# Key projections of a cross-attention kernel: whole block products in four banks instead of Strassen's products with a chain of reads

## The chip, the cores and the metric

The kernel runs on one core of one Trainium2 chip. The metric is the device time of one execution in microseconds (us); before the change the median of three runs is 1877.12 us (1876.99 to 1877.57). Engines are named as in the profile: PE is TensorE (PEld its weight loads), DVE is VectorE, ACT is ScalarE, POOL is GpSimd, SP is SyncE, which issues most DMAs.

## The reference

For each of B = 32 batches, x and ctx (here y) are 256 x 1024 (channels C x positions N):

```
x_q = w_qk y            (as N x C)        x_k = w_qk x          x_v = w_v x + b_v
energy = x_q x_k        (N x N)           attention = softmax over the last axis
attention = attention / (1e-7 + its sum over the rows)
x_r = x_v attention     (C x N)           out = x + relu(w_t (x - x_r) + b_t)
```

## The kernel before

**What is computed.** The kernel folds weights once, at the start. The query and the key share w_qk, so it forms G = -(w_qk^T w_qk) and multiplies only x by it; these 256 x 1024 products are called the keys. The energies of a batch are then y^T times its keys, with their sign turned, so that exp takes a scale of -1. Likewise w_t w_v is folded into the values, and w_t x is a product of its own, the x product.

**Forms.** Full precision is had from two reduced-precision forms of every operand, HIGH and LOW (the rounded value and the rest). A product of 128 x 128 by 128 x 512 is three matmuls in ORDER: high by high, high by low, low by high. The second needs the right operand's LOW form, the third the left operand's. HIGH forms are made by ACT (copy with rounding), LOW forms by POOL or DVE (a subtraction).

**Strassen's products.** Keys, x product and each of four energy groups (E0 to E3, 256 rows each) are 2 x 2 block products done with seven block products P1 to P7 instead of eight. `chain` (line 335) makes the words `kP1` to `kP7`, `xP1` to `xP7` and `E0P1` to `E3P7`. The partial sums P1, P1 + P6 and P1 + P6 + P7 grow in one bank, "a", and each is copied out by ACT (`r1`, `r2`, `r3`) before the next product may add to it; DVE joins a copy with bank "b" or "c" (`c11`, `c22`, `c12`, `c21`); P3 goes into bank "c" once `c22` has read it.

**Keys (lines 344 to 383).** KB puts the key's a, b and c into banks 2, 0 and 1. `kc11`, `kc22` write blocks 11 and 22 to `sums`, `kc12` leaves block 12 in its bank, block 21 is in bank 2 after P4. Then follow the forms of what the energies read: `khD`, `klD` for blocks 11 and 22, `kh21`, `kl21` for block 21, and four sums `kT1` to `kT4` with their forms `kTh0`, `kTl0` (of T1 and T3) and `kTh1`, `kTl1` (of T2 and T4). Of these `kT1`, `kT3`, `kT4` and `kl21` are on DVE, `kT2`, `klD`, `kTl0` and `kTl1` on POOL, the rest on ACT.

**Banks.** There are eight PSUM banks. Energies use 0 to 3 (a = 3, b = 0, c = 1, d = 2). A row tile n of 128 rows has its 1024 energies in banks 2 and 3 (n odd) or 0 and 1 (n even): `exp{n}` on ACT in place with the row sum, `ri{n}` on DVE, and for each half h `h{n}{h}` (HIGH of the probabilities, ACT), `l{n}{h}` (LOW, DVE) and `sum{n}{h}` (share of the column sum, DVE). When those three have read a half, its bank is free. Banks 4 to 7 take the values (`V..`, 12 matmuls of 256 columns each), the x product, and then the attention products `A{n}{c}{h}` (three matmuls each). The key products of batch b+1 are made at the end of batch b, and so have to wait for the last tiles, 6 and 7, to leave banks 0 to 2.

**Order.** The order of all work is written out by hand as words in three texts: FIRST (batch 0), STEADY (batches 1 to 29, with + and - for words of the next and the last batch) and LAST. Each engine executes its words in the order of the text (`InOrder`, line 51); waits between engines follow from the data. `ldx`, `ldy` and `st` are DMAs on SP's queue, `add` one on POOL's. Loads go through a ring of two buffers (`raws`), sums through one of four, reads through one of four (`rs`). `ys..`, `yl..`, `ysl..`, `xl..`, `xTl..` and `join..` are POOL's other work, `yh..`, `ysh..`, `xh..`, `xTh..`, `pos..` ACT's; `cols`, `inv`, `turn`, `div..` (DVE) make the column sums and divide by them.

**Batch 0** makes its keys another way: `first_keys` (line 578) multiplies whole blocks by the untransformed forms of G, `gt`, in four banks at once (words `FHH0` to `FHL1`), while `left_blocks("G", ...)` makes the seven left operands that Strassen's products need from batch 1 on (words `Gs1` to `GlS`). `whole` (line 589) makes a block of the first energies and x products from six matmuls: three forms by two halves of the contraction. `Ssq` multiplies w_v by w_t for the values, `Swtc` copies the turned w_t that it reads.

Of the kernel before, what the change touches and what calls it, by code (L numbers as in the profile page):

```python
# [17 lines left out]
def kernel(  # L18
# [135 lines left out]
    def graw():  # L154
        return split(rs["g"])


    gt, tt = (
        efs["weights"][:, j].rearrange("p h (k c) -> p h k c", k=KC) for j in range(FORMS)
    )  # L160
# [68 lines left out]
    for k in range(KC):  # L229
        once(f"Sgh{k}", act.mul, gt[:, HIGH, k], g_bank[:, k], -1.0)  # L230
    once(
        "Sgl", dve.scalar_tensor_tensor, gt[:, LOW], g_bank, -1.0, value(gt[:, HIGH]),
        ALU.mult, ALU.subtract,
    )
    once("Sgraw", lambda: act.mul(graw(), g_bank, -1.0))
# [342 lines left out]
    def first_keys(j, m, k):  # L578
        for i in range(KC):
            for h in range(MH):  # L580
                matmul(
                    (kb["b"], kb["c"], kb["a"], banks[:, 3])[2 * i + h],
                    gt[:, j, k, ts(i, P)],
                    xf[:, m, 2 * k + h],
                    (j, m, k) == (HIGH, HIGH, 0),
                    (j, m, k) == (LOW, HIGH, 1),
                )

    def whole(into, left, right):
        for j, m in ORDER:  # L590
            for k in range(KC):
                matmul(
                    into, left(j, k), right(m, k),
                    (j, m) == ORDER[0] and k == 0, (j, m) == ORDER[-1] and k == KC - 1,
                )
# [25 lines left out]
    forms("k11", lambda j: g(j, K11), kb["b"])  # L621
    forms("k22", lambda j: g(j, K22), banks[:, 3])
    forms("k12", lambda j: k12[:, j], kb["c"])
    words["Fraw11"] = lambda b: act.copy(sums["k", b][:, 0], kb["b"])
    words["Fraw22"] = lambda b: act.copy(sums["k", b][:, 1], banks[:, 3])
# [121 lines left out]
    for c in range(KC):  # L747
# [19 lines left out]
        FX11 E1P6 h01 Gs1 yl10 h00 E1r2 FX00 kTl0 E1P7 +ldx0 l00 l01 l10 Fxw1 sum00 E1r3
        E1P5 E1P4 +xh0 E1c22 Gs2 E1c21 E1P2 Fxw0 E1P3 A100 Gl12 Gs4 Ts1 yl11 exp3 E1c11
        Gs3 Ts3 ri3 E1c12 h31 ysl1 Ts2 exp2 A110 l31 sum31 A101 +ldx1 A010 A111 +xl0 GhS
        ri2 E2P1 h21 A001 E2r1 sum30 sum21 l21 h20 E2P6 +xT3 Ts4 +xT1 l20 +ldy0 E2P5 E2r2  # L770
        h30 sum20 l30 E2P7 E2P2 E2P4 E2r3 A011 +xh1 E2c22 E2P3 +xT2 A301 GlS A000 A201
        A300 E2c21 A311 E2c11 exp5 ri5 E2c12 h51 l51 sum51 exp4 +yh01 ri4 E3P1 sum50 h41
        E3r1 h40 +xT4 h50 A211 E3P6 E3r2 l41 sum41 l40 l50 E3P5 E3P7 +xTh1 E3r3 E3P4 sum40
        E3P2 A310 E3c22 E3c21 E3P3 +xTh0 +xl1 +ys01 +ys02 +yl01 A210 +ys04 +xTl1 exp7
        +yh00 E3c11 A511 ri7 +ldy1 E3c12 h70 exp6 l70 sum70 ri6 A510 A200 A501 ThS h61
        +kP1 sum71 A410 l61 +kr1 sum61 +kP6 +xTl0 h60 +ys03 +kr2 +ysh0 TlS +kP5 sum60 +kP7
        A401 l60 +kP2 +ys11 +kr3 +yl00 cols +kc22 +kP3 A411 A500 +kc11 +kc12 +ys12 h71
        +ysl0 +kP4 +ys14 A400 +khD +yh10 +kT1 +ys13 l71 +kT2 A701 +klD +kT4 inv +kT3 A710
# [21 lines left out]
        -kTh1 -kh21 -kTh0 -yh11 --A700 -E0P1 -E0r1 -kTl1 --A611 --A600 -E0P6 -kTl0 -ysl1  # L800
        --turn --A610 -kl21 -E0P2 -E0r2 -E0P7 -E0P5 --div0 -E0r3 -E0P4 --div1 -E0c11 -yl11
        -E0c22 -E0c21 -exp1 -ri1 -yl10 -V11 -E0P3 -h11 -h10 -E0c12 -sum11 -l11 -V10 -l10
        -exp0 -vh1 -ri0 -V01 -E1P1 -sum10 -E1r1 -h01 -V00 -vl1 -l01 -sum01 --join0 -E1P6
        -vh0 -E1r2 -h00 -xP1 -E1P4 -E1P7 --join1 -vl0 ldx0 -l00 -E1P5 -sum00 xh0 -xP2
        -A111 -E1r3 -E1c22 -E1P2 -E1c21 -xr1 --pos0 -E1c11 -xc11 -exp3 -xP6 -E1P3 -xr2
        -ri3 xT1 -xP5 -xP7 -A011 -A100 -h31 -E1c12 -sum31 -l31 -exp2 -h30 -ri2 -xr3 -E2P1
        -A311 -h21 -E2r1 -xP4 -E2P6 -sum30 -l30 -xc22 -xP3 -sum21 -l21 xl0 --add0 xT2 xT3
        -E2P4 -h20 -xw21 -E2r2 -E2P7 -xc12 -l20 -sum20 xh1 -E2r3 -E2P5 -E2c22 xT4 -A110
        xTh1 -E2c21 -E2P2 -E2c11 xl1 -exp5 -E2P3 -A101 -ri5 -A000 -A010 -h51 -A001 -A300
        -E2c12 -sum51 -exp4 -l51 -ri4 -h40 -E3P1 -h41 -E3r1 xTh0 -A200 -A310 -sum50 -l40  # L810
        -l41 -sum41 ldy0 ldy1 -E3P6 -E3r2 -E3P5 -sum40 ys03 -E3P7 -h50 ys11 yh00 ys01
        -A210 xTl1 -l50 -E3P4 -E3r3 --pos1 -E3c22 -E3c21 -exp7 -A301 -E3P2 -E3c11 -ri7
        -E3P3 yl00 ys02 xTl0 -E3c12 ys04 yh10 -h70 -A510 -A500 -A211 -A201 --add1 -sum70
        -l70 -exp6 -ri6 kP1 -sum71 -h60 -A511 -h61 -A410 -sum61 ys13 kr1 yh01 -h71 -l61
        kP6 -l71 -l60 kr2 --st1 yl01 Zx0 --st0 -sum60 kP5 kP7 -A411 ysh0 kr3 ysl0 kP2 kc22
        kc11 kP3 kc12 khD -A400 -A710 kP4 kT1 -A610 -A501 -A711 -A401 kT3 -cols kT2 klD
# [61 lines left out]
```

## Time and profile before

| | |
|---|---|
| median of three runs | 1877.12 us |
| the profiled execution | 1876.58 us, its span 1874.5 us |
| PE busy | 1861.9 us, 8680 matmuls |
| weight loads (PEld) | 1506.3 us |
| DVE, ACT, POOL busy | 1596.7, 1439.3, 1407.3 us |
| granted TensorE clock, mean | 0.999 |
| DMA | 136.75 MB, mean 73 GB/s |

Times in rows of the profile are us; the mean of one instruction is ns. A row of the order of time has start, duration, engine, line, operation, tiles written <- read, and count; a bracket gives the idle time before it and what ended that. In a group, the number behind the second bar is the idle time before its instructions and what ended most of it. All kernel work goes through one helper, so its line is L62 and groups are told apart by tiles: `xf,gws` are the keys, `gf,ysum` and `gf,yd` the energies, `xf,tws` the x product, `vws,xf` the values, `efs,uf` the attention. Matmuls are pipelined, so that the duration shown for one (some 390 ns) is longer than the step from one to the next.

### The profile page before, as it was taken

How to read it: one execution, taken by the hardware profiler on the slowest of the kernel's cores; microseconds unless marked ns; L12 is line 12 of the kernel's file. 1: busy time of each engine (PE TensorE's matmuls, PEld its weight loads, DVE VectorE, ACT ScalarE, POOL GpSimd, SP SyncE). 2: the span in 40 equal slices, each digit the busy share in tenths (PEclk: the TensorE clock that was granted, in tenths of full speed). 3: DMA queues.
4: the chain of work that ended last, by engine and by line, in shares of the span. 5: the costliest groups of instructions: out<-in, count | busy, mean ns of one | idle time of the engine just before them, and what ended most of it. 6: DMA issues, size and time to landing. Idle time of an engine off the chain costs nothing.

```text
span 1874.5 us, 25084 instructions
## 1 busy us (share of the span) xinstructions
PE 1861.9 (99%) x8680; PEld 1506.3 (80%) x8680; DVE 1596.7 (85%) x3044; ACT 1439.3 (77%) x2223; POOL 1407.3 (75%) x975
## 2 busy tenths in 40 slices
...
GB/s 97 39 76 90 58 89 57 68 90 68 80 68 60 88 75 72 68 68 79 90 58 79 57 79 90 57 89 53 74 91 60 88 56 68 90 68 79 74 62 68
DMA packets 46719, 136.75 MB, mean 73 GB/s; under 512 B 4480, under 2 KB 5376, under 8 KB 46592
## 3 DMA queue, kind: packets, MB, share of 16 engines
...
## 4 chain that ended last, share of the span: by engine, by line
PE 94%; DVE 2%; ACT 1%; issue 1%; POOL 1%; DMA 0%; DVEq 0%; ACTq 0%
PE banks L62 94%; DVE sums L62 1%; ACT rs L62 1%; POOL xf L62 0%; DVE banks L62 0%; POOL sums L62 0%; ACT banks L62 0%; DVE acc L62 0%; DVE efs L62 0%; DMA z<-in_L_xattn_w_qk_dram 0%; POOL raws L62 0%; ACT efs L62 0%; POOL z L62 0%; POOL yd L62 0%; DMA out_dram<-z 0%
## 5 line engine op out<-in xcount | busy, mean ns | idle before, releaser
L62 PE MATMUL banks<-efs,uf 128*128 128x512 f32 x3072 | 771.7, 390 | 0.0
L62 PEld LDWEIGHTS banks<-efs,uf 128*128 128x128 f32 x3072 | 576.5, 188 | 124.6 <-ACT xe L62 0.3
L62 ACT COPY rs<-banks 128x512 f32<-128x512 f32 (+1 forms) x475 | 279.2, 588 | 202.5 <-PE banks L62 193.1
L62 PE MATMUL banks<-gf,ysum 128*128 128x512 f32 x1524 | 415.1, 394 | 0.0
L62 DVE SCALAR_TENSOR_TENSOR efs<-banks,small,efs 128x512 fp32r<-128x512 f32 x512 | 374.5, 742 | 11.2 <-ACT efs L62 9.7
L62 ACT ACTIVATE efs<-banks,small 128x512 fp32r<-128x512 f32 x512 | 340.0, 690 | 43.7 <-DVE small L62 31.8
L62 ACT ACTIVATE banks<-banks,small 128x1024 f32<-128x1024 f32 x256 | 279.2, 1091 | 82.8 <-DVE small L62 79.1
L62 DVE SCALAR_TENSOR_TENSOR acc<-banks,small,acc 128x512 f32<-128x512 f32 x448 | 325.1, 743 | 17.5 <-ACT efs L62 15.2
L62 PEld LDWEIGHTS banks<-gf,ysum 128*128 128x128 f32 x1524 | 276.7, 188 | 72.2 <-ACT rs L62 14.9
L62 PE MATMUL banks<-gf,yd 128*128 128x512 f32 x1158 | 330.4, 397 | 0.5 <-DVE acc L62 0.2
L62 DVE CUSTOM_DVE_ANT_0 banks<-banks,rs 128x512 f32<-128x512 f32 x254 | 178.6, 703 | 117.3 <-PE banks L62 81.9
L62 POOL TENSOR_TENSOR sums<-raws 128x256 f32<-128x256 f32 (+1 forms) x188 | 190.1, 1064 | 116.7 <-DMA raws<-in_ctx_dram 116.6
L62 PEld LDWEIGHTS banks<-gf,yd 128*128 128x128 f32 x1158 | 207.8, 188 | 62.1 <-issue 10.4
L62 POOL TENSOR_TENSOR gf<-sums,gf 128x1024 fp32r<-128x1024 f32 x95 | 227.3, 2408 | 2.3 <-ACT gf L62 0.2
L62 POOL TENSOR_TENSOR xf<-sums,xf 128x1024 fp32r<-128x1024 f32 x62 | 147.9, 2408 | 97.6 <-ACT xf L62 97.5
L62 PEld LDWEIGHTS banks<-vws,xf 128*128 128x128 f32 x1536 | 196.6, 190 | 8.2
L62 DVE CUSTOM_DVE_ANT_0 banks<-banks,rs,small 128x512 f32<-128x512 f32 x254 | 192.2, 757 | 11.8
L62 PE MATMUL banks<-vws,xf 128*128 128x256 f32 x1536 | 198.7, 282 | 0.0
L62 POOL TENSOR_TENSOR z<-z,xe 128x1024 f32<-128x1024 f32 x62 | 149.1, 2405 | 61.8 <-DVE z L62 61.8
L62 PE MATMUL banks<-xf,gws 128*128 128x512 f32 x651 | 179.6, 407 | 4.1 <-DVE sums L62 0.4
L62 PE MATMUL banks<-xf,tws 128*128 128x512 f32 x651 | 173.3, 390 | 0.0
L62 POOL TENSOR_TENSOR ysum<-sums,ysum 128x1024 fp32r<-128x1024 f32 x64 | 154.6, 2416 | 21.5 <-ACT ysum L62 21.5
...
## 6 DMA issues: line engine op xcount, KB each, us to landing
...
```

What stands on the lines that cost most here:

```text
L62: self.last = getattr(self.engine, name)(*args, **kwargs)
```

## The change

The keys of batches 1 to 31 are made as whole blocks: `key_product(i, h)` makes block (i+1, h+1) from six matmuls (words `kD11`, `kD12`, `kD21`, `kD22`), each in a bank of its own: KB is now 11 in bank 2, 12 in bank 0, 21 in bank 1, 22 in bank 3. No partial sum is read on the way. ACT copies blocks 11 and 22 to `sums` (`kraw11`, `kraw22`); `kT1`, `kT3` read block 12 from bank 0, `kT4`, `kh21`, `kl21` block 21 from bank 1. Batch 0 uses the same banks and the same forms of G, kept now in `gws`, and the seven left operands of G are no longer made. All three orders are written anew.

```diff
-    gws = mem.tile([P, FORMS, LEFTS, P], F32R, name="gws")
+    gws = mem.tile([P, FORMS, KC, C], F32R, name="gws")
...
-    once("Sgraw", lambda: act.mul(graw(), g_bank, -1.0))
...
-    left_blocks("G", gws, graw)
     left_blocks("T", tws, lambda: wtT)
...
-    KB = dict(a=2, b=0, c=1)
-    chain("k", KB, lambda i: lambda j: gws[:, j, LEFT[i]], lambda i: lambda m: xf[:, m, RIGHT[i]])
+    def whole(into, left, right):
+        for j, m in ORDER:
+            for k in range(KC):
+                matmul(
+                    into, left(j, k), right(m, k),
+                    (j, m) == ORDER[0] and k == 0, (j, m) == ORDER[-1] and k == KC - 1,
+                )
+
+    KB = {11: 2, 12: 0, 21: 1, 22: 3}
     kb = {w: banks[:, at] for w, at in KB.items()}
+
+    def key_product(i, h):
+        whole(
+            kb[10 * (i + 1) + h + 1],
+            lambda j, k: gws[:, j, k, ts(i, P)],
+            lambda m, k: xf[:, m, 2 * k + h],
+        )
...
-    def key_read(b, j):
-        act.copy(rs["k", b, j], kb["a"])
-
-    def key_block(b, j, w, to):
-        into = kb[w] if to is None else sums["k", b][:, to]
-        dve.tensor_tensor(into, kb[w], rs["k", b, j], ALU.add)
+    def key_raw(b, at):
+        act.copy(sums["k", b][:, at], kb[11 * (at + 1)])
...
-    for j in range(1, 4):
-        word(f"kr{j}", key_read, j)
-    word("kc11", key_block, 1, "b", 0)
-    word("kc22", key_block, 3, "c", 1)
-    word("kc12", key_block, 2, "c", None)
-    word("kh21", lambda b: act.copy(g(HIGH, K21), kb["a"]))
+    for i in range(2):
+        word(f"kraw{11 * (i + 1)}", key_raw, i)
+        for h in range(2):
+            once(f"kD{i + 1}{h + 1}", key_product, i, h)
+    word("kh21", lambda b: act.copy(g(HIGH, K21), kb[21]))
...
-    word("kT1", key_sum, ("k13", 0), "c", ("k", 0))
-    word("kT3", key_sum, ("k13", 1), "c", ("k", 1))
+    word("kT1", key_sum, ("k13", 0), 12, ("k", 0))
+    word("kT3", key_sum, ("k13", 1), 12, ("k", 1))
...
-    word("kT4", key_sum, ("k24", 1), "a", ("k24", 0))
+    word("kT4", key_sum, ("k24", 1), 21, ("k24", 0))
...
     FIRST = """
-        Fxh0 Sgram Scorner Sgh0 Stp Sgh1 Swt Fxl0 Swtc FHH0 FHL0 Ssq ys01 ys03 Sgl xh1
-        Sbvw ys02 FHH1 yh00 yh01 Fyh Sgraw ys04 Fxl1 FLH0 FLH1 FHL1 ldy1 Th12 Svh Gh12 Sth
-        Th22 Fraw11 Fkh12 Svl yl01 Fraw22 kT1 kT3 ysh0 Gh22 Fkh22 kh21 yh10 Tl12 Fkl22
...
+        ys03 Fxh0 Sgram Sgh0 Scorner Swt Swtc Stp Th22 Sgh1 Th12 Ssq ys01 Fxl0 xh1 ys02
+        Sgl FHH0 FHL0 FHH1 yh01 Sth Fyh FLH0 Svh ldy1 Fxl1 Svl FLH1 FHL1 Fyl V01 V00 yl01
+        Tl12 Fkh11 kraw11 Fkh22 kh21 Sbvw Fkl11 kT1 kraw22 ys04 kl21 kT2 Fkh12 Fkl22 FE10
...
     STEADY = """
-        E0P1 -A611 -turn kTh1 kh21 E0r1 kTh0 kl21 -A610 kTl1 -A700 kTl0 E0P6 E0r2 yh11
-        E0P4 E0P2 E0P7 E0r3 -div1 E0c11 E0P5 E0c22 -A600 V10 E0c21 exp1 E0P3 V11 -div0 ri1
-        E0c12 h11 h10 vh1 -join1 -join0 exp0 sum11 l11 sum10 yl11 V01 E1P1 yl10 vl1 ysl1
-        V00 E1r1 ri0 h01 E1P6 vh0 xP1 E1r2 +ldx0 l10 sum00 sum01 l01 vl0 E1P4 E1P7 E1P5
-        h00 xr1 E1r3 l00 -pos1 +xh0 E1c22 xP6 xP2 E1c21 exp3 E1P2 E1c11 xc11 xP5 E1P3 A111
-        ri3 xr2 h31 E1c12 A100 xP7 exp2 sum31 l31 ri2 sum30 A011 xr3 E2P1 xc22 h21 E2r1
-        l21 xP4 xP3 E2P6 h30 h20 E2r2 -add1 +xT1 A311 +xh1 +xT2 sum21 sum20 xc12 l30 E2P5
-        E2P7 l20 E2r3 xw21 -pos0 E2c22 +xT4 E2P4 E2c21 A000 E2P2 A101 E2P3 A110 +xT3 E2c11
-        exp5 ri5 A211 A010 A001 h51 E2c12 sum51 l51 E3P1 A310 A301 +xl0 h50 +xl1 -st1
-        +ldy0 exp4 ri4 +yh00 h41 E3r1 l50 sum41 E3P6 h40 E3r2 l41 E3P5 sum50 l40 +ys01
-        E3P7 E3P4 A300 A210 +xTh1 +ys02 +ldy1 +xTl1 sum40 E3r3 E3c22 +yh01 E3c21 +xTh0
-        +xTl0 E3P2 E3P3 E3c11 A511 -add0 +ys04 +ys11 exp7 A200 A411 A201 ri7 E3c12 h70 l70
-        exp6 sum70 ri6 h61 +ys03 +kP1 +yh10 A510 A501 sum71 sum60 +kr1 sum61 l61 h60 +yl00
-        +kP6 +kP5 h71 +ys12 l71 +kr2 l60 +ys14 +yl01 +ys13 +kP7 +kr3 +kc22 +kP2 +kc11
-        +ysh0 A401 +kP3 +ysh1 +khD +kP4 A711 +ysl0 A701 A500 A410 A400 A601 A710 +kc12
-        +kT1 ++ldx1 cols +kT2 -st0 +kT3 +kT4 inv +klD
+        E0P1 E0r1 kh21 -A701 -A700 -A610 kTl1 E0P6 E0r2 kTl0 -A600 -A601 E0P7 E0r3 kl21
+        -div1 E0P5 -div0 E0c22 E0P4 E0P2 E0c21 ysh1 E0c11 E0P3 V11 V10 yl11 -join0 ysl1
+        yl10 +xT1 exp1 ri1 E0c12 +ldx1 h11 V01 exp0 vh1 sum11 l11 E1P1 ri0 h00 sum10 h10
+        E1r1 V00 E1P6 vl1 h01 sum00 l10 l01 sum01 l00 xP1 E1P4 E1r2 vh0 E1P7 vl0 E1P5 xr1
+        E1r3 +xh0 +xT3 +xl0 -join1 E1P2 xP2 A111 xP6 E1c22 E1c21 E1c11 E1P3 exp3 xr2 xc11
+        ri3 E1c12 +ldy0 h31 -pos0 xP5 xP7 A011 l31 xr3 exp2 A311 sum31 xc22 ri2 E2P1 sum30
+        A100 E2r1 h21 h30 xP3 sum20 sum21 l21 +ys01 +xT2 xc12 l30 E2P6 E2r2 h20 A000 xP4
+        +xh1 l20 E2P7 E2P5 E2P4 E2P2 A300 A101 +ys02 E2r3 E2c22 E2P3 E2c21 E2c11 xw21
+        +xTh0 +ys04 +ys03 +xTl0 +xT4 +xl1 +ldy1 exp5 +yh00 A110 A200 ri5 h51 E2c12 exp4
+        +ysh0 l51 sum51 ri4 A001 A010 h41 A310 E3P1 h40 A211 A210 E3r1 sum41 h50 +xTh1
+        E3P6 l40 l41 sum50 E3r2 A301 sum40 E3P5 l50 E3P7 -pos1 E3r3 +yh01 -add1 A500 E3P4
+        +xTl1 +ys11 -add0 E3P2 E3c22 E3c21 +yl00 +ys12 E3c11 E3P3 A511 A510 A201 A501 A410
+        E3c12 exp7 ri7 +yh10 h71 sum70 sum71 +ys13 +ys14 +yl01 +ysl0 l71 exp6 h70 ri6 A411
+        sum60 l70 h60 l60 +kD22 +kD11 +kraw22 h61 +kD12 A401 l61 sum61 +kD21 A711 +kraw11
+        +yh11 +kT1 +kT2 +khD A611 A400 cols +kT4 inv +kT3 turn +kTh1 +klD A710 -st0 -st1
+        ++ldx0 +kTh0
     """
...
```

LAST holds the same kinds of words as STEADY, for the last two batches, and the output of the last.

More of the change, by code (lines that the diff above doesn't have):

```diff
@@ L152, in product_t @@
         return split(rs["product"])
[L154 to L160, printed above, removed]
+    tt = efs["weights"][:, HIGH].rearrange("p h (k c) -> p h k c", k=KC)
     k12 = efs["blocks"][:, HIGH]
@@ L229 @@
     for k in range(KC):
[L230 removed]
+        once(f"Sgh{k}", act.mul, gws[:, HIGH, k], g_bank[:, k], -1.0)
     once(
[L232 removed]
+        "Sgl", dve.scalar_tensor_tensor, gws[:, LOW], g_bank, -1.0, value(gws[:, HIGH]),
         ALU.mult, ALU.subtract,
     )
[L235 removed]
     once("Swt", turned_wt)
@@ L581, in first_keys @@
                 matmul(
-                    (kb["b"], kb["c"], kb["a"], banks[:, 3])[2 * i + h],
-                    gt[:, j, k, ts(i, P)],
+                    kb[10 * (i + 1) + h + 1],
+                    gws[:, j, k, ts(i, P)],
                     xf[:, m, 2 * k + h],
@@ L586, in first_keys @@
                     (j, m, k) == (LOW, HIGH, 1),
[L587 to L594, printed above, removed]
                 )
@@ L619, in forms @@
         )
[L621 to L625, printed above, removed]
+    forms("k11", lambda j: g(j, K11), kb[11])
+    forms("k22", lambda j: g(j, K22), kb[22])
+    forms("k12", lambda j: k12[:, j], kb[12])
     def y21_from():
@@ L767 @@
[L767 to L778, printed above, removed]
@@ L779 @@
-        A711 ++ldx1 A601 +ysh1
+        ys03 Fxh0 Sgram Sgh0 Scorner Swt Swtc Stp Th22 Sgh1 Th12 Ssq ys01 Fxl0 xh1 ys02
+        Sgl FHH0 FHL0 FHH1 yh01 Sth Fyh FLH0 Svh ldy1 Fxl1 Svl FLH1 FHL1 Fyl V01 V00 yl01
+        Tl12 Fkh11 kraw11 Fkh22 kh21 Sbvw Fkl11 kT1 kraw22 ys04 kl21 kT2 Fkh12 Fkl22 FE10
+        yh10 vh0 kT3 Fkl12 yl10 ysh0 yh00 yh11 FE11 kTh0 kT4 Stl Fmin1 exp1 yl00 vl0 kTh1
+        ysl0 kTl1 ys11 ri1 V10 kTl0 FE01 FE00 V11 h11 ys13 sum10 sum11 l11 ys12 Sbias vh1
+        FX01 E1P1 Fmin0 exp0 vl1 E1r1 ri0 h01 h00 FX00 +ldx0 l01 l00 sum01 E1P6 E1r2 FX11
@@ new lines @@
+        E1P7 E1P5 FX10 h10 E1r3 Fxw0 l10 sum00 E1c22 E1P4 E1P3 E1P2 yl11 ys14 Ts3 A101
+        ysh1 E1c21 Ts1 Fxw1 exp3 A100 A001 E1c11 ri3 +ldx1 A111 h31 h30 E1c12 l31 sum31
+        exp2 A000 E2P1 sum30 ri2 A011 +xh0 E2r1 h21 ysl1 +xT1 sum21 A301 l21 E2P6 A110 h20
+        E2r2 E2P7 +xT2 Tl22 +xT3 E2r3 +xl0 l20 E2P5 l30 sum20 E2P4 +xT4 A201 E2c22 E2P2
+        E2P3 A010 A311 A211 A310 E2c21 A210 +xh1 +xTh1 E2c11 exp5 ri5 h51 +ldy0 E2c12
+        +yh01 l51 sum51 +xl1 +ys01 +ys03 exp4 +ys02 Ts2 ri4 E3P1 h50 sum41 l50 h40 A300
@@ L780 @@
+        E3r1 E3P6 h41 sum50 +xTl1 +yl01 E3r2 A510 E3P7 E3r3 +yh00 l41 Ts4 +yl00 ThS E3P5
+        +xTh0 E3P4 sum40 l40 E3c22 +ldy1 E3c21 E3P2 E3c11 E3P3 TlS exp7 E3c12 ri7 A511
+        A200 A501 A401 +ys11 +xTl0 sum71 +ys04 +ys12 h70 A500 A411 exp6 l70 sum70 ri6 h71
+        +ys14 +yh11 +ys13 h60 sum61 +kD11 l71 +kD22 l60 +ysh0 sum60 +kD12 h61 +kraw11 l61
+        +kD21 A410 +ysl0 +yh10 +kraw22 +kT1 +kT2 +khD cols +kT4 inv +kT3 turn +klD A711
+        A400 A710 A611 ++ldx0 +kTh1 +kTh0
     """
@@ L798 @@
+        +yh11 +kT1 +kT2 +khD A611 A400 cols +kT4 inv +kT3 turn +kTh1 +klD A710 -st0 -st1
+        ++ldx0 +kTh0
     """
     LAST = """
[L800 to L816, printed above, removed]
@@ L817 @@
-        -A700 kT4 kTh1 kh21 -inv kl21 kTl1 E0P1 -A600 -turn -A611 kTh0 E0r1 yh11 kTl0
-        -A701 -div1 E0P6 E0r2 -A601 E0P2 E0P7 -div0 E0P5 E0P4 E0c11 E0r3 E0c22 -join0
-        E0c21 V00 exp1 ri1 h10 E0P3 sum11 h11 E0c12 l11 V10 V11 exp0 l10 ri0 vh1 sum01
-        E1P1 V01 vl1 sum10 E1r1 h01 ys12 yl11 ys14 E1P6 vh0 E1P4 E1r2 ysh1 l01 sum00 yl10
-        vl0 E1P7 E1r3 h00 -pos0 E1P5 E1c22 l00 xP1 A111 xr1 E1c21 E1P3 exp3 E1P2 E1c11 xP5
-        xP6 ri3 E1c12 h31 -join1 l31 xr2 h30 sum31 A011 xP2 xP7 exp2 l30 E2P1 A311 sum30
```

46 lines of the change are left out of this document (33 added, 13 removed).

## The prediction

> **What bounds the kernel now.** I read the page first (busy shares, chain, costliest groups), then groups by shape, then the orders of time of one batch for each engine, because every batch from 1 to 29 is issued from the same written order.
>
> ```profile
> span 1874.5 us, 25084 instructions
> PE 1861.9 (99%) x8680; PEld 1506.3 (80%) x8680; DVE 1596.7 (85%) x3044; ACT 1439.3 (77%) x2223; POOL 1407.3 (75%) x975
> PE 94%; DVE 2%; ACT 1%; issue 1%; POOL 1%; DMA 0%; DVEq 0%; ACTq 0%
> ```
>
> TensorE carries 94% of the chain that ended last. Its 99% is no measure of room, as matmul ends are modelled; what counts is the time from one start to the next. These are TensorE's runs in one batch (start, duration, tiles, count), from the last energy chain to the next batch's first energy product:
>
> ```profile
> 916.79 1.75 PE L62 MATMUL banks<-efs,uf 128*128 128x512 f32 x7
> 918.51 0.94 PE L62 MATMUL banks<-gf,yd 128*128 128x512 f32 x3
> 919.28 1.53 PE L62 MATMUL banks<-efs,uf 128*128 128x512 f32 x6
> 920.65 2.50 PE L62 MATMUL banks<-gf,ysum 128*128 128x512 f32 x9
> 922.99 0.86 PE L62 MATMUL banks<-gf,yd 128*128 128x512 f32 x3
> ...
> 926.43 2.88 PE L62 MATMUL banks<-efs,uf 128*128 128x512 f32 x12
> 929.34 0.93 PE L62 MATMUL banks<-xf,gws 128*128 128x512 f32 x3
> 930.11 1.52 PE L62 MATMUL banks<-efs,uf 128*128 128x512 f32 x6
> 931.47 3.17 PE L62 MATMUL banks<-xf,gws 128*128 128x512 f32 x12
> 934.47 0.84 PE L62 MATMUL banks<-efs,uf 128*128 128x512 f32 x3
> 935.42 1.66 PE L62 MATMUL banks<-xf,gws 128*128 128x512 f32 x6
> 936.91 4.92 PE L62 MATMUL banks<-efs,uf 128*128 128x512 f32 x21
> 941.67 0.86 PE L62 MATMUL banks<-gf,yd 128*128 128x512 f32 x3
> ...
> 950.71 3.03 PE L62 MATMUL banks<-vws,xf 128*128 128x256 f32 x24
> 953.58 0.93 PE L62 MATMUL banks<-gf,yd 128*128 128x512 f32 x3
> ```
>
> The 21 undisturbed attention matmuls take 941.67 - 936.91 = 4.76 us: a pitch of 0.2267 us, so a product of three costs 0.68. The 24 value matmuls take 2.87 us, 0.1196 each. A batch has 222 of the first and 48 of the second: 56.07 us without a wait. One whole batch, from E0P1 to E0P1:
>
> ```profile
> 883.71:941.67 57.96, 57.83 (x271) 46.84 (x270) 49.68 (x96) 44.90 (x70) 44.09 (x31) 1.00 0.29 73
> ```
>
> So TensorE loses 57.96 - 56.07 = 1.89 us a batch to waits, at a granted clock of 1.00, and VectorE, ScalarE and GpSimd have 8 to 14 us to spare. Against the pitch, the key products lose 0.96 of this: entry to kP1 0.19 (926.43 + 12 x 0.2267 = 929.15, seen 929.34) and 0.09 in it (0.77 for 0.68); kP6, kP5, kP7, kP2 take 3.00 for 2.72, loss 0.28; entry to kP3 0.27 (0.95 for 0.68) and 0.13 in kP3 and kP4. The weight loads of these products show the reason, in the same stretch and in total:
>
> ```profile
> 929.31 0.53 PEld L62 LDWEIGHTS banks<-xf,gws 128*128 128x128 f32 x3 [0.42 <-ACT banks L62]
> 932.98 1.22 PEld L62 LDWEIGHTS banks<-xf,gws 128*128 128x128 f32 x6 [0.41 <-ACT rs L62]
> 935.41 1.23 PEld L62 LDWEIGHTS banks<-xf,gws 128*128 128x128 f32 x6 [0.52 <-DVE sums L62]
> L62 PEld LDWEIGHTS banks<-xf,gws 128*128 128x128 f32 x651 | 114.7, 188 | 63.0 <-DVE sums L62 16.5 <-ACT rs L62 13.3 <-ACT banks L62 13.1
> ```
>
> Three waits: kP1 for the release of bank 2 by the last tile, kP7 for the read kr2 of the running sum, kP3 for kc22 to free bank 1. The totals (42.9 us of idle loads, 1.38 a batch against 1.35 here) say that all 31 key stages look alike. Another 0.52 lies in the last energy chain: E3P1 0.13 + 0.09 (916.79 + 7 x 0.2267 = 918.38, seen 918.51; then 0.77 for 0.68), and E3P6, E3P5, E3P7 take 2.34 for 2.04, 0.30.
>
> **The change, part by part.** *Matmuls.* Seven products of three become four of six: 24 for 21. In 31 batches 93 are added, all on the chain; at the pitch 93 x 0.2267 = **+21.1 us**. The load of weights, 188 ns, is no price between: it already runs beneath the pitch. The Trainium skill speaks against taking TensorE as full: "Perfetto Trace Analysis", Identifying the Most-Contended Engine, judges it by the share of weight loads, here 80%, by which the 93 could hide and the sum be 21 us lower. The rows disagree: with 188 in 226.7 ns of undisturbed stream the loads are busy 83% when nothing is left to fill.
>
> *The chain of reads.* The reads kr1 to kr3 and the joins kc11, kc22, kc12 go; two raw copies come:
>
> ```profile
> L62 ACT COPY rs<-banks 128x512 f32<-128x512 f32 x474 | 278.9, 588 | 199.8 <-PE banks L62 190.4 <-DVE efs L62 0.3
> L62 DVE TENSOR_TENSOR sums<-banks,rs 128x512 f32<-128x512 f32 x62 | 40.1, 687 | 35.5 <-ACT rs L62 34.0 <-POOL sums L62 1.6
> L62 ACT COPY sums<-banks 128x512 f32<-128x512 f32 x2 | 1.2, 598 | 0.7 <-PE banks L62 0.7
> ```
>
> ScalarE saves 3 x 0.588 - 2 x 0.598 = 0.57 us a batch, VectorE three joins of 0.687 = 2.06. Neither is the bound, so that is worth nothing by itself. What counts is that no key product waits for a read any more: the waits of kP7 and kP3, 0.68, have no counterpart. The wait at the entry turns on when the last tiles free their banks; now four banks are needed instead of three. Rows for that way, from E3P7 (started 922.17):
>
> ```profile
> 923.18 0.59 ACT L62 COPY rs<-banks 128x512 f32<-128x512 f32 x1
> 923.80 0.70 DVE L62 CUSTOM_DVE_ANT_0 banks<-banks,rs 128x512 f32<-128x512 f32 x1 [0.82 <-ACT rs L62]
> 924.71 0.76 DVE L62 CUSTOM_DVE_ANT_0 banks<-banks,rs,small 128x512 f32<-128x512 f32 x1
> 925.56 1.09 ACT L62 ACTIVATE banks<-banks,small 128x1024 f32<-128x1024 f32 x1 [0.32 <-DVE small L62]
> 926.58 0.19 ACT L62 ACTIVATION_READ_ACCUMULATOR banks<-banks,small 128x1 f32 x1
> 927.78 0.75 DVE L62 SCALAR_TENSOR_TENSOR efs<-banks,small,efs 128x512 fp32r<-128x512 f32 x1
> 928.45 0.74 DVE L62 SCALAR_TENSOR_TENSOR acc<-banks,small,acc 128x512 f32<-128x512 f32 x1
> ```
>
> The joins follow each other at 0.91, exp takes 1.2, a split or share on VectorE 0.66 behind another. E3P7 starts at 0: read 0.9 to 1.5, c22 1.5, c21 2.4, c11 3.3, c12 4.25 to 5.1, exp7 3.25 to 4.5, yh10, h71 to 5.55, exp6 to 6.7; VectorE ri7, sum70, sum71, l71 to 7.3, ri6, sum60, l70 to 8.7, l60 to 9.35. TensorE after E3P7: ten products (A500 E3P4 E3P2 E3P3 A511 A510 A201 A501 A410 A411), so kD22 (bank 3) at 11 x 0.68 = 7.48, kD11 (bank 2) 8.85, kD12 (bank 0) 10.2. Adding 0.15 from VectorE's end to a matmul (sum70 ended 929.19, kP1 started 929.34), the banks come free at 7.45, 8.85 and 9.5: the first two in time by hundredths, the third by 0.7, so I take **-0.96 a batch, 31 x 0.96 = -29.8 us**; its bounds are 0.68 (the entry wait of 0.28 stays, -21.1) and 0.96.
>
> *Order.* E3P7 waited because only E3P5, 0.68, stood between E3P6 and E3P7: read and hand-over need 0.68 + 0.30 = 0.98. The new order has A301 and E3P5 there, 1.36, and everywhere at least two products or one value block (six matmul pairs, 1.43) between P1, P6 and P7. E3P1 needs sum51: from E2P3's start c12 0.95 later takes 0.85, l51 0.66, sum51 0.74, hand-over 0.15, together 3.35, and now E2P3 and five attention products, 4.08, lie ahead of it. So **-0.52 a batch, -16.1 us** (bounds 0 and -16.1). New: E2P1 needs sum31 behind ri3, E1c12, l31 on VectorE, and ri3 waits for exp3; from E1P3's start 1.15 + 0.85 + 0.66 + 0.74 + 0.15 = 3.55 to 3.6 against the five products E1P3, xP5, xP7, A011, A311, 3.40: I take 0.2 a batch, **+6.2 us** (bounds 0 and 0.5, +15.5, a wait as long as the raw key waits above).
>
> *The next batch's first products.* E0P1's second matmul needs klD, POOL's split behind kT2 behind kT1:
>
> ```profile
> 937.15 0.69 DVE L62 TENSOR_TENSOR sums<-banks,sums 128x512 f32<-128x512 f32 x1
> 938.08 1.29 POOL L62 TENSOR_TENSOR sums<-sums 128x512 f32<-128x512 f32 x1
> 939.32 7.26 POOL L62 TENSOR_TENSOR gf<-sums,gf 128x1024 fp32r<-128x1024 f32 x3
> ```
>
> From kT1's start to klD's end 939.32 + 2.42 - 937.15 = 4.59. In the new order kT1 can start 0.17 after kD12; A401, kD21, A711, A611, A400, A710 are 7 x 0.68 = 4.76 behind it and the second matmul 0.23 more: 4.82 against 4.59 + 0.1. Enough by 0.1; kTl1 and kTl0 follow at 2.42 each, and E0P6 and E0P7 stand 2.72 and 4.76 behind E0P1. Cost 0 while POOL reaches kT2 in time. E0P5 (bank 1) now stands behind kl21, which ends 2 us earlier.
>
> *Start.*
>
> ```profile
> 6.53 2.07 PE L62 MATMUL banks<-xf,efs 128*128 128x512 f32 x8
> 8.44 1.89 PE L62 MATMUL banks<-z 128*128 128x256 f32 x8
> 6.81 0.59 ACT L62 COPY z<-banks 128x512 f32<-128x512 f32 x1
> ```
>
> Ssq (eight matmuls at 8.44) moves ahead of the first keys (eight at 6.53), but needs Swtc, the copy that ends at 7.40: TensorE stands about 1 us, **+1.0** (bounds -1 and +3, as the rest of the first and last order is new). The sixteen small G forms that leave the first batch run beside TensorE: nothing.
>
> **Sum**: 21.1 - 29.8 - 16.1 + 6.2 + 1.0 = -17.6 us. The profiled execution took 1876.58 (span 1874.5 and 2.1 around it), 0.54 under the median of the runs, 1877.12: 1859.0 + 0.5 = **1859.5 us**, 0.94% faster.
>
> **Rivals.** *Gain given away (same).* The bank releases, ready by hundredths, come late and E3's gain is eaten by new waits of its size: keys then win 0.68 and pay 0.68. Time 1877 + 1 = 1878. For it: three of the deadlines above (kD22, kD11, klD) have 0.1 us of slack or less; against: the covers between P1, P6 and P7 are longer in the text itself.
>
> *Slower: POOL late at kT2.* Between kD21 and E0P1 stand four products, 2.72, where seven, 4.76, stood behind kP4. POOL must do add1, xTl1, ys11, add0, yl00, ys12, ys13, ys14, yl01, ysl0 ahead of kT2; xTl1 and ysl0 cost 2.42 each like klD. I lay its end 0.5 before kT2's turn. Beyond 0.5 + 0.1 each us late is 31 us. It decides from 0.6 + 17.6/31 = 1.2 us late; 1.5 late, less than one more split of 2.42 in the way, gives 1859.5 + 31 x 0.9 = 1887. For: POOL idles for y blocks, 116.6 us in 30 waits:
>
> ```profile
> POOL sums L62 <- DMA raws<-in_ctx_dram: 116.6, 30, 4.1
> ```
>
> Against: in 57.96 us POOL works only 44.09.
>
> *All waits gone.* The period falls to 56.07 + 0.68 = 56.75: 31 x 1.21 = 37.5 less, 1840. For: VectorE has 2.06 more room; against: E2P1 above.
>
> *Matmuls cheaper than their pitch.* If the added ones ran at the load's 0.188, 93 x 0.039 = 3.6 less: 1856. Against: no undisturbed run above falls below 0.2267. The Trainium skill ("TensorE: Matmul & The Clock Gate", Back-to-back issue gap) gives about 131 ns for sustained 512 columns, by which the 93 would be, as an estimate, 12.2 us and the time 1851; the rows disagree by 96 ns a matmul.
>
> **How the numbers follow.** Forecast 0.50 (1852 to 1868 by the bounds of E2P1 and start), all waits gone 0.20, gain given away 0.13, slower 0.15, cheaper matmuls 0.02. About 0.2%, 3.75 us, is what can be told from no change. The first, second and last are faster, with a little of the third: 0.75; same 0.10; slower 0.15. The range 1845 to 1877 leaves out half of the slowest and the lowest of the fastest.
>
> **What would show it.** After: key matmuls 744 and all 8773; the weight loads of the keys idle for neither reads nor joins, TensorE's key run of 12 in 2.72; E3P6 to E3P7 without idle; E2P1 waiting for VectorE by 0.2; batch 57.4. I am wrong if the loads of energy products wait for POOL's key forms, or if the entry to the keys still waits for the tiles.

## The result

The changed kernel takes **1843.65 us** (1843.48 to 1843.87) against 1877.31 us: a ratio of 0.9821, with a 95% interval of 0.9804 to 0.9838. The forecast was 1859.5, with a range from 1845 to 1877. The sign was right; the gain, 33.7 us, is nearly twice the 17.6 forecast and 1.4 us outside the range. The nearest of the cases was the rival "all waits gone", 1840, which had been given 0.20.

The page of the changed kernel, its span and its first line of busy times, and the groups of TensorE's weight loads by shape:

```profile
span 1842.1 us, 25248 instructions
PE 1833.0 (100%) x8773; PEld 1538.3 (84%) x8773; DVE 1554.1 (84%) x2951; ACT 1404.7 (76%) x2188; POOL 1398.7 (76%) x968
...
L62 PEld LDWEIGHTS banks<-gf,ysum 128*128 128x128 f32 x1524 | 282.4, 188 | 61.2 <-ACT rs L62 2.5 <-DVE efs L62 0.2
L62 PEld LDWEIGHTS banks<-gf,yd 128*128 128x128 f32 x1158 | 212.9, 188 | 48.2 <-POOL gf L62 6.4 <-ACT banks L62 0.7 <-issue 0.3
...
L62 PEld LDWEIGHTS banks<-xf,gws 128*128 128x128 f32 x768 | 144.0, 188 | 30.1
```

The two energy groups in the kernel before, for comparison:

```profile
L62 PEld LDWEIGHTS banks<-gf,ysum 128*128 128x128 f32 x1524 | 276.7, 188 | 72.2 <-ACT rs L62 14.9 <-POOL gf L62 5.9 <-DVE acc L62 0.7
L62 PEld LDWEIGHTS banks<-gf,yd 128*128 128x128 f32 x1158 | 207.8, 188 | 62.1 <-issue 10.4 <-DVE efs L62 7.0 <-POOL gf L62 3.6
```

There are 93 more matmuls and a shorter span. The key loads have no releaser left: 30.1 us over 768 loads is 39 ns each, the 226.7 - 188 by which a load is shorter than the pitch. Before, 42.9 us of their idle time were waits. The energy products' waits for ScalarE's reads fell from 14.9 to 2.5 us. What grew is the wait of the `gf,yd` products for POOL's key forms, from 3.6 to 6.4 us.

One batch from E0P1 to E0P1 (TensorE, its loads, VectorE, ScalarE and POOL), and TensorE's runs around the keys in it:

```profile
868.14:925.00 56.86, 56.86 (x275) 47.84 (x273) 48.34 (x93) 43.81 (x68) 43.87 (x31) 1.00 0.27 75
```

```profile
906.64 0.84 PE L62 MATMUL banks<-gf,ysum 128*128 128x512 f32 x3
907.32 0.84 PE L62 MATMUL banks<-efs,uf 128*128 128x512 f32 x3
908.00 1.52 PE L62 MATMUL banks<-gf,ysum 128*128 128x512 f32 x6
...
912.08 4.24 PE L62 MATMUL banks<-efs,uf 128*128 128x512 f32 x18
916.16 4.24 PE L62 MATMUL banks<-xf,gws 128*128 128x512 f32 x18
920.24 0.84 PE L62 MATMUL banks<-efs,uf 128*128 128x512 f32 x3
920.92 1.52 PE L62 MATMUL banks<-xf,gws 128*128 128x512 f32 x6
922.28 2.88 PE L62 MATMUL banks<-efs,uf 128*128 128x512 f32 x12
925.00 0.91 PE L62 MATMUL banks<-gf,yd 128*128 128x512 f32 x3
```

This batch takes 56.86 us instead of 57.96, where the matmuls alone need 56.07 + 0.68 = 56.75. The mean from the E0P1 of batch 1 to that of batch 29 is 56.92 us (71.04 to 1664.82); in the kernel before it was 58.00 (71.89 to 1695.79). The 18 key matmuls before A401 take 4.08 us, the pitch exactly. E3P6, A301 and E3P5 follow without a gap. From E3P7 (908.68) to E0P1 are 16.32 us; before, 922.17 to 941.67, 19.50. Behind E3P7 lay 16 attention products before, 12 now: of the other four, three stand among the energies and one behind E0P1.

### The profile page after: what moved, and what is told of

Its sections match the earlier page's. It is cut to its first block, busy times and chain, and to the rows that moved or that the text cites. A ratio compares the mean times of both kernels' runs of the same rounds, so it can differ in the third digit from the quotient of the medians.

```text
span 1842.1 us, 25248 instructions
## 1 busy us (share of the span) xinstructions
PE 1833.0 (100%) x8773; PEld 1538.3 (84%) x8773; DVE 1554.1 (84%) x2951; ACT 1404.7 (76%) x2188; POOL 1398.7 (76%) x968
## 5 line engine op out<-in xcount | busy, mean ns | idle before, releaser
L62 PE MATMUL banks<-gf,ysum 128*128 128x512 f32 x1524 | 409.5, 390 | 0.0
L62 DVE SCALAR_TENSOR_TENSOR acc<-banks,small,acc 128x512 f32<-128x512 f32 x448 | 330.2, 745 | 46.2 <-ACT efs L62 41.5
L62 PEld LDWEIGHTS banks<-gf,ysum 128*128 128x128 f32 x1524 | 282.4, 188 | 61.2 <-ACT rs L62 2.5
L62 ACT COPY rs<-banks 128x512 f32<-128x512 f32 (+1 forms) x382 | 224.7, 588 | 123.0 <-PE banks L62 119.6
L62 PE MATMUL banks<-gf,yd 128*128 128x512 f32 x1158 | 314.1, 392 | 0.3 <-DVE small L62 0.3
L62 POOL TENSOR_TENSOR sums<-raws 128x256 f32<-128x256 f32 (+1 forms) x188 | 200.0, 1064 | 112.4 <-DMA raws<-in_x_dram 65.1
L62 PEld LDWEIGHTS banks<-gf,yd 128*128 128x128 f32 x1158 | 212.9, 188 | 48.2 <-POOL gf L62 6.4
L62 POOL TENSOR_TENSOR xf<-raws,xf 128x1024 fp32r<-128x1024 f32 x62 | 149.2, 2406 | 79.2 <-ACT xf L62 79.2
L62 POOL TENSOR_TENSOR xf<-sums,xf 128x1024 fp32r<-128x1024 f32 x62 | 157.9, 2547 | 44.2 <-ACT xf L62 44.2
L62 ACT CAST gf<-sums 128x1024 fp32r<-128x1024 f32 x95 | 100.0, 1053 | 117.9 <-DVE sums L62 117.9
```

The lines of the kernel that those rows point to most:

```text
L62: self.last = getattr(self.engine, name)(*args, **kwargs)
```

## Experiments

**The added matmuls by themselves.** Three more matmuls ahead of kD21 in every batch, their sum thrown away:

```diff
     def key_product(i, h):
+        if (i, h) == (1, 0):
+            product(kb[21], lambda j: gws[:, j, 0, ts(1, P)], lambda m: xf[:, m, 0], True)
         whole(
```

> The kernel after, with three more matmuls of 512 columns ahead of kD21 in each of 31 batches; their sum is thrown away, since kD21 starts its bank anew. The price of the added matmuls by itself. At the pitch of 0.2267: 93 x 0.2267 = 21.1, less up to 2 for the wait of E0P1 that this covers: 1863 to 1865 us. At 131 ns, which the Trainium skill (TensorE: Matmul & The Clock Gate, Back-to-back issue gap) gives for sustained work: 1856. Hidden in idle weight loads: 1844.

Measured: 1860.4 us. One batch, and the loads of the energies' first group:

```profile
875.94:933.41 57.47, 57.47 (x277) 48.56 (x276) 48.37 (x93) 43.86 (x68) 43.95 (x31) 1.00 0.29 74
...
L62 PEld LDWEIGHTS banks<-gf,yd 128*128 128x128 f32 x1158 | 215.3, 188 | 43.8 <-ACT banks L62 0.6 <-issue 0.3
```

The batch shown grows by 0.61, the mean batch by 0.55 (56.92 to 57.47), and the waits for POOL (6.4 us in all) are gone, covered by the added work. With the batch at 57.47 and 225 + 3 wide and 48 narrow matmuls, the pitch sum is 57.43: the added matmuls cost their whole pitch. Their net price, 16.8 us, lies 2.6 to 4.6 below what I expected, because the cover was worth 0.68 - 0.55 = 0.13 a batch, 4 us in 31 batches, and I had allowed 2. The Trainium skill ("TensorE: Matmul & The Clock Gate", Back-to-back issue gap) gives 131 ns a matmul of 512 columns for a sustained stream; this trace does not agree, at 226.7 ns. The Trainium skill ("Perfetto Trace Analysis", Identifying the Most-Contended Engine) judges TensorE's headroom by the achieved share of its peak rate and by the busy share of the weight loads; here that busy share, 80% before and 84% now, shows no room, as 188 of 226.7 ns, 83%, is what a stream without waits gives.

**Block products alone.** The changed code with the order of before; each block product stands where a Strassen product stood. In STEADY, the key words up to kT1 and the attention products among them:

```diff
-  +kP1 A510 A501 +kr1 +kP6 +kP5 +kr2 +kP7 +kr3 +kc22 +kP2 +kc11 A401 +kP3 +kP4 A711 A701 A500 A410 A400 A601 A710 +kc12 +kT1
+  +kD11 A510 A501 +kD21 +kraw11 +kD12 A401 +kD22 A711 +kT1 A701 +kraw22 A500 A410 A400 A601 A710
```

> Block products alone, in the order of before: each kD stands where the Strassen product that used its bank stood, the raw copies where the reads were. Theory A (the chain of reads cost the keys their waits, the order is a second, separate gain): the keys still wait 0.28 for the last tile's bank at their entry and some 0.2 at kD12 for l60; the other waits of before, 0.93 a batch, stay. Batch 56.75 + 0.48 + 0.93 = 58.16, 30 x 0.20 more than before: 1883 us (1869 if the entry doesn't wait). Theory B (the new order made the whole gain, blocks only cost their 93 matmuls and the old waits stay): 1877 + 21 = 1898 us. Theory C (blocks made the gain, through free banks and a lighter VectorE, which takes the other waits away as well): 1850 us or less.

It took 1880.1 us, a ratio of 1.0015 to the kernel before (1.0006 to 1.0024). But in this version batch 0's copy of block 11 overwrites a buffer that its T forms still need, so what it computes is wrong. The second version has that copy behind the T forms (TlS) and is otherwise the same:

> Block products in the order of before once more, with batch 0's copy of block 11 behind the T forms that its buffer would overwrite; batches 1 to 31 as in the first such run, which took 1880.1 us. Theory A (blocks take the waits of kP7 and kP3 away and pay them back as matmuls; all other waits of before belong to the order): 1880 us again. Theory C (the lighter VectorE takes the other waits away): 1850 us or less.

Measured: 1879.32 us, ratio 1.0013 (1.0004 to 1.0022). One batch, one of the longest (the mean is 58.04, from 72.80 to 1697.94), and the loads:

```profile
886.16:944.46 58.30, 58.07 (x274) 47.63 (x273) 47.92 (x93) 44.54 (x68) 43.95 (x31) 1.00 0.28 73
...
L62 PEld LDWEIGHTS banks<-gf,ysum 128*128 128x128 f32 x1524 | 276.7, 188 | 72.7 <-ACT rs L62 15.0 <-POOL gf L62 6.5 <-DVE acc L62 0.7
L62 PEld LDWEIGHTS banks<-gf,yd 128*128 128x128 f32 x1158 | 209.7, 188 | 62.0 <-issue 10.5 <-DVE efs L62 7.0 <-POOL gf L62 1.9
L62 PEld LDWEIGHTS banks<-xf,gws 128*128 128x128 f32 x768 | 140.4, 188 | 44.4 <-ACT banks L62 13.2 <-DVE efs L62 0.9 <-ACT ysum L62 0.4
```

The key waits for reads and joins (13.3 and 16.5 us before) are gone; that for the last tile's bank, 13.1, stays at 13.2. The energies' waits are almost those of before: 15.0 for reads (14.9), 7.0 for `efs` (7.0), 10.5 at `issue` (10.4), 6.5 and 1.9 for POOL's forms (5.9 and 3.6), although VectorE is lighter by the joins. So **blocks in the old order pay their gain back as matmuls and are 0.13% slower; a lighter VectorE takes no wait away**. By itself, in the order of before, the change of algorithm wins nothing.

**Strassen with better covers for an energy.** In the kernel before, one attention product moved:

```diff
-  E3P6 E3r2 E3P5 E3P7 E3P4 A300 A210
+  E3P6 E3r2 E3P5 A300 E3P7 E3P4 A210
```

> The kernel before, with A300 moved from behind E3P4 to between E3P5 and E3P7 in batches 1 to 29, so that E3P7 has two products of cover as in the new order. Theory A (products that can cover are a fixed stock; one put there is missing between E3P7 and kP1): E3P7 saves 0.30, the last tile is ready 0.38 later and kP1 waits 0.68 more: 29 x 0.38 = 11 us slower, 1888. Theory B (the old order simply had a wait that reordering removes): 29 x 0.30 less, 1868.5 us.

Measured: 1886.79 us, 9.4 more than the kernel before. The loads:

```profile
L62 PEld LDWEIGHTS banks<-gf,ysum 128*128 128x128 f32 x1524 | 279.0, 188 | 62.2 <-POOL gf L62 6.1 <-ACT rs L62 2.7 <-DVE acc L62 0.7
...
L62 PEld LDWEIGHTS banks<-xf,gws 128*128 128x128 f32 x651 | 114.7, 188 | 82.4 <-ACT banks L62 32.4 <-DVE sums L62 16.6 <-ACT rs L62 13.4
```

The energies' wait for reads goes from 14.9 to 2.7 us as in the new order, and the keys' wait for the last tile grows from 13.1 to 32.4. The wait went where the cover was taken from.

**Strassen with better covers for the keys.** Again in the kernel before:

```diff
-  +kP6 +kP5 +kr2 +kP7 +kr3 +kc22 +kP2 +kc11 A401 +kP3 +kP4 A711 A701 A500 A410 A400 A601 A710
+  +kP6 +kP5 +kr2 A500 +kP7 +kr3 +kc22 +kP2 +kc11 A401 A410 +kP3 +kP4 A711 A701 A400 A601 A710
```

> The kernel before, with A500 moved ahead of kP7 and A410 ahead of kP3 in batches 1 to 29. Theory A (stock of covers): kP7 and kP3 save 0.68, but from kP3 to E0P1 only five products are left where kc12, kT1, kT2, klD need 6.3 us from kP3's start: E0P1 waits 1.4; 29 x 0.7 slower, 1897 us. Theory B (order alone): 29 x 0.68 faster, 1857 us.

Measured: 1893.6 us, 16.2 more.

```profile
L62 PEld LDWEIGHTS banks<-gf,yd 128*128 128x128 f32 x1158 | 207.5, 188 | 97.7 <-POOL gf L62 40.3 <-issue 10.5 <-DVE efs L62 7.0
...
L62 PEld LDWEIGHTS banks<-xf,gws 128*128 128x128 f32 x651 | 119.1, 188 | 39.7 <-ACT banks L62 14.0 <-DVE sums L62 1.2 <-ACT rs L62 1.2
```

The keys' waits for reads and joins fall from 29.8 to 2.4 us, and E0P1 waits for POOL's klD, 40.3 us for 3.6. In this order the products behind E3P7 are a stock that the kernel had spent in full.

**Strassen in the new order.** In batches 1 to 29 all but the keys as in the changed kernel, with kP1 to kP4 where the blocks stand. The words that free the banks of tiles 6 and 7 had to be sorted anew, too:

```diff
-  A410 A411 +kD22 +kD11 +kraw22 +kD12 A401 +kD21 A711 +kraw11 +kT1 +kT2 +khD A611 A400 ... +klD A710
+  A410 +kP1 A411 +kr1 +kP6 +kr2 +kP5 +kP7 +kr3 +kc22 +kP2 A401 +kc11 +kP3 +khD +kP4 A400 +kc12 +kT1 +kT2 A711 ... A611 ... +klD ... A710
```

> The kernel before with Strassen's seven key products, but with the new order for everything else in batches 1 to 29; the key words stand where the block products stand, with the covers A411, A401, A400, A711, A611, A710 among and behind them. Theory A (the new order lives on the covers that block products set free, 12 attention products behind E3P7 instead of 16): the waits of E1 to E3 go, but E0P1 waits 2 to 3 us for klD and the keys wait about 1: batch 59 to 59.6, 29 x 1.1 to 1.6 more than before, 1909 to 1924 us. Theory B (the order is what brought the gain, and Strassen's keys would do better in it by three matmuls): 29 x 0.68 under the kernel after, 1824 us.

Measured: 1940.97 us, ratio 1.0346. The loads around the keys of one batch:

```profile
962.24 0.53 PEld L62 LDWEIGHTS banks<-xf,gws 128*128 128x128 f32 x3 [0.60 <-ACT banks L62]
...
963.88 1.24 PEld L62 LDWEIGHTS banks<-xf,gws 128*128 128x128 f32 x6 [0.42 <-ACT rs L62]
965.53 0.53 PEld L62 LDWEIGHTS banks<-xf,gws 128*128 128x128 f32 x3 [0.41 <-ACT rs L62]
967.23 0.53 PEld L62 LDWEIGHTS banks<-xf,gws 128*128 128x128 f32 x3 [1.18 <-DVE efs L62]
...
974.85 0.30 PEld L62 LDWEIGHTS banks<-gf,yd 128*128 128x128 f32 x2 [2.07 <-POOL gf L62]
```

E0P1 waits 2.07 for klD, as laid out; the 1.18 at kP2 (for tile 6, `l60`) was not, and at 29 batches it is more than the 17 us beyond my range. It comes of how the words were sorted here: on VectorE `sum71` and `l71` (964.45 to 965.77) stand ahead of `sum60` and `l60`, which ends at 967.17, although the bank 3 that they free takes no product of Strassen's keys. In starts, the wait at kP2 is 1.02 a batch in the mean, 30 us in 29 batches; without it the kernel would take some 1911 us, as an estimate, still more than before. This is one arrangement, not the best there can be: it shows that this order does not carry Strassen's keys, not that none would.

**One read put back.** In the changed kernel, ScalarE copies bank 1 in the middle of kD21:

```diff
-  +kD21 A711 +kraw11
+  +kDa +kq +kDb A711 +kraw11
```

(kDa, kDb: the first and last three matmuls of kD21; kq: the copy.)

> The kernel after, with one read of a running sum put back in batches 1 to 29: ScalarE copies bank 1 after the first three matmuls of kD21, and the last three wait for it, with no other work in between. The result is unchanged. Theory A (a read and its hand-over cost 0.98 us when nothing covers them, as E3P6 to E3P7 showed in the kernel before): 29 x (0.98 - 0.1 for E0P1's wait, which it covers) = 26 us more, 1869 us. Theory B (a read of a running sum is cheap, and the old waits came from the order): under 1850 us.

Measured: 1908.77 us, 65 more instead of 26.

```profile
951.56 0.64 PEld L62 LDWEIGHTS banks<-xf,gws 128*128 128x128 f32 x3
953.30 0.53 PEld L62 LDWEIGHTS banks<-xf,gws 128*128 128x128 f32 x3 [1.10 <-ACT rs L62]
...
958.28 0.30 PEld L62 LDWEIGHTS banks<-gf,yd 128*128 128x128 f32 x2 [1.48 <-POOL gf L62]
```

The read's own wait is there: loads 1.74 apart instead of 0.68, 0.95 in matmul starts. But kraw11 stood behind kq on ScalarE, and with it khD and klD, so that E0P1 waits too. So kq was put behind kraw11:

```diff
-  +kDa +kq +kDb A711 +kraw11
+  +kDa +kraw11 +kq +kDb A711
```

> The kernel after with the one read of bank 1 in the middle of kD21 again, but now behind kraw11 in ScalarE's order, so that it no longer holds up the copy of block 11. Theory A (an uncovered read of a running sum costs 0.95 to 0.98 us, and the other 1.3 us of the first such run were kraw11 standing behind the read): 29 x (0.95 - 0.07) = 25 us over the kernel after, 1869 us. Theory B (the read itself delays what follows by more, through E0P1): 1890 us or more.

Measured: 1878.91 us, 35 over the changed kernel, between both theories: in the mean batch, the read costs 0.95 again and E0P1 loses 0.22 more. ScalarE's order in one batch, and E0P1's load:

```profile
941.80 0.59 ACT L62 COPY rs<-banks 128x512 f32<-128x512 f32 x1 [2.13 <-PE banks L62]
942.28 0.62 ACT L62 CAST yd<-raws 128x512 fp32r<-128x512 f32 x1
942.80 1.06 ACT L62 CAST gf<-sums 128x1024 fp32r<-128x1024 f32 x1
```

```profile
942.44 0.53 PEld L62 LDWEIGHTS banks<-xf,gws 128*128 128x128 f32 x3 [1.10 <-ACT rs L62]
...
946.40 0.30 PEld L62 LDWEIGHTS banks<-gf,yd 128*128 128x128 f32 x2 [0.44 <-POOL gf L62]
```

khD (942.80, ended 943.86) still stands behind the read, and klD (2.4 us on POOL) behind it, which brings E0P1's load to 946.40. A read in this chain has two prices: 0.95 us on TensorE, and everything queued behind it on ScalarE.

**The wait that was left.** Two edits at E0P1, whose second load waited 0.21 in the batch shown. One gives block 12 later:

```diff
-  +kD22 +kD11 +kraw22 +kD12 A401 +kD21
+  +kD22 +kD11 +kraw22 A401 +kD12 +kD21
```

> The kernel after, with A401 ahead of kD12 instead of behind it in batches 1 to 29, so that block 12 comes 0.68 us later and everything else on TensorE stays. Theory A (kT1 waits now for ysl0, until 0.3 us after block 12 is there): 29 x (0.68 - 0.3) = 11 us more, 1855 us. Theory B (the chain kT1, kT2, klD to E0P1 is bound by block 12 alone, with 0 to 0.1 to spare): 29 x 0.58 to 0.68 = 17 to 20 us more, 1861 to 1863 us. Theory C (E0P1 has room): 1843.6 us.

Measured: 1857.8 us, 14.2 more, 0.49 for each of 29 batches: between A and B, with 0.19 of 0.68 to spare. The other moves POOL's DMA:

```diff
-  E3P7 -pos1 E3r3 +yh01 -add1 A500 E3P4 +xTl1
+  E3P7 -pos1 E3r3 +yh01 A500 E3P4 +xTl1 -add1
```

> The kernel after, with the word -add1 (POOL's DMA that waits for ScalarE's relu of the batch before) behind +xTl1 instead of ahead of it, in batches 1 to 29. Theory A (POOL idles 3.9 us at this DMA, ends ysl0 late, kT1 waits for ysl0 because it takes over its buffer, and klD is 0.1 late for E0P1): the rest of the wait goes, 29 x 0.07 to 0.13 = 2 to 4 us less, 1840 to 1841.6 us. Theory B (E0P1's rest comes from kD12 and the chain kT1, kT2, klD alone): 1843.6 us.

Measured: 1840.47 us, ratio 0.9809 (0.9796 to 0.9822), 3.2 under the changed kernel. E0P1's load, that DMA, ysl0 with the split ahead of it, and kT1 in the changed kernel, then kT1 and one batch with the edit:

```profile
925.18 0.30 PEld L62 LDWEIGHTS banks<-gf,yd 128*128 128x128 f32 x2 [0.21 <-POOL gf L62]
...
909.36 0.88 POOL L62 DMA_DIRECT2D z<-in_x_dram  x1 [3.85 <-ACT z L62]
...
916.45 1.85 POOL L62 TENSOR_TENSOR yd<-raws,yd 128x512 fp32r<-128x512 f32 x1
917.70 2.97 POOL L62 TENSOR_TENSOR ysum<-sums,ysum 128x1024 fp32r<-128x1024 f32 x1
...
920.70 0.69 DVE L62 TENSOR_TENSOR sums<-banks,sums 128x512 f32<-128x512 f32 x1 [0.36 <-POOL ysum L62]
```

```profile
918.27 0.69 DVE L62 TENSOR_TENSOR sums<-banks,sums 128x512 f32<-128x512 f32 x1 [0.20 <-PE banks L62]
...
865.93:922.74 56.81, 56.81 (x275) 47.99 (x273) 48.37 (x93) 43.81 (x68) 43.82 (x31) 1.00 0.26 75
```

kT1 waited for POOL, whose ysl0 (the row at 917.70) ended at 920.67, because its sum takes over a buffer of the ring of four; with the edit it waits for block 12 alone, and E0P1 no more. The batch is within 0.06 of its matmuls.

**The start.** The same, with Ssq behind FHL0 in batch 0 as before the change:

```diff
-  Th12 Ssq ys01 Fxl0 xh1 ys02 Sgl FHH0 FHL0 FHH1
+  Th12 ys01 Fxl0 xh1 ys02 Sgl FHH0 FHL0 Ssq FHH1
```

> The kernel with -add1 behind +xTl1, and in batch 0 also Ssq behind FHL0 again, as in the kernel before. Theory A (Ssq ahead of the first keys keeps TensorE standing for Swtc): 1 us less than the kernel with -add1 moved alone, which took 1840.5: 1839.5 us. Theory B (the first stage is made up for later in batch 0, where the values and E1 wait for other things): 1840.5 us.

Measured: 1839.17 us, ratio 0.9801 (0.9788 to 0.9815): 1.3 under the kernel without this edit, less than these times can tell apart. The first value matmuls, which follow the last key of batch 0, with `-add1` moved alone and with both edits:

```profile
14.48 1.72 PE L62 MATMUL banks<-vws,xf 128*128 128x256 f32 x13
```

```profile
13.72 2.56 PE L62 MATMUL banks<-vws,xf 128*128 128x256 f32 x20
```

The first keys are done 0.8 us earlier, in keeping with theory A. In the changed kernel's own profile these matmuls begin at 15.10, but there the work ahead of Ssq is late already, so that the difference to it is not the edit's alone. Both edits together are the fastest kernel measured here.

## Why the prediction went wrong, step by step

- **Matmuls, +21.1.** Right: the pitch was measured by itself.
- **The chain of reads, -29.8.** Right in size and place: no key load waits. The bank entry was in time as laid out, with more room: l71 ended at 915.70 and kD22 began at 916.16. (The key run has 18 matmuls, not the 12 I named, as kD12 too stands ahead of A401.) But what I booked for the entry, 0.28 of it, the blocks did not bring alone: with blocks in the old order the entry waits as before, 13.2 us.
- **Order, E3, -16.1.** Right: E3P6 to E3P7 without a gap. The reason I gave, that the order has more covers, was half of it. The covers come from the keys, as the three runs with Strassen's keys show.
- **The step that failed is "New: E2P1 ... 0.2 a batch, +6.2 us", and with it what the sum left out.** Of 1.89 us of waits it dealt with 0.96 and 0.52; the other 0.41 a batch, some 13 us, it let stand without a word, while it added a new wait. In the changed kernel the new wait does not come, and of all waits 0.11 is left in the batch shown. For E2P1, ri3, c12, l31 and sum31 on VectorE:

```profile
889.43 0.16 DVE L62 RECIPROCAL small<-small 128x1 f32<-128x1 f32 x1
889.84 0.76 DVE L62 CUSTOM_DVE_ANT_0 banks<-banks,rs,small 128x512 f32<-128x512 f32 x1 [0.24 <-PE banks L62]
...
890.59 0.75 DVE L62 SCALAR_TENSOR_TENSOR efs<-banks,small,efs 128x512 fp32r<-128x512 f32 x1
891.25 0.74 DVE L62 SCALAR_TENSOR_TENSOR acc<-banks,small,acc 128x512 f32<-128x512 f32 x1
```

  E1P3 began at 888.96. c12 came 0.88 behind it, not 1.15, and l31 0.75 behind c12, not 0.85; sum31 ended at 891.99, 0.37 under my 3.55 with its hand-over, and E2P1 began at 892.36, five products behind E1P3, unhindered. The larger part, 0.27, is c12's start: the prediction names ri3 and exp3 ahead of it, but ri3 was done and VectorE had been idle for 0.24 when TensorE's P3, which c12 needs, was done. The other 0.10 is that VectorE starts l31 as c12 ends, where I had laid down a longer c12.

  The rows show part of what the 0.41 was: 5.9 us for POOL's forms in the `gf,ysum` loads (all at E0P7) and 7.0 for `efs` in the `gf,yd` loads (nearly all at E2P4). With blocks in the old order both stay, 6.5 and 7.0; in the changed kernel they are gone. So they went by the new order. In matmul starts, E0P7, E2P4 and E1P1 lose 0.05 to 0.08 a batch each before the change, 0.21 together, and under 0.02 each after it. The rest is spread over the batch in steps too small to name a cause.
- **Sum of it.** 31 x (0.20 + 0.41 - 0.11 left) = 15.5 us, of the 16 between forecast and result. The mean batches say nearly the same: 58.00 to 56.92 is 1.08 less, where the terms add up to 0.96 + 0.52 - 0.68 - 0.20 = 0.60.
- **E0P1, cost 0.** Nearly: 0.1 a batch, by the mechanism of the slower rival (POOL late, through ysl0), but through kT1's buffer and far below its price.
- **Start, +1.0.** Of the right size for the first keys: moving Ssq back brings them 0.8 us earlier. But batch 0 as a whole did not grow: E0P1 of batch 1 begins at 71.04 us, before the change at 71.89. One batch's share of the other terms would be 0.60 of these 0.85, which leaves the start near nothing, inside its bounds.
- **The chances.** "All waits gone" was the better reading: the covers counted in the new text spoke for it, and against it only E2P1, a reckoning finer than its error. Its 1840 lay below the range that I gave.
